# A planner's constants and priorities set anew, and one queue in it for all transfers

## The chip, the core and the metric

The kernel runs on one core of one Trainium2 chip. The core has five engines with an instruction list each, executed in order: TensorE (PE in the profile, with its weight loads shown apart as PEld), VectorE (DVE), ScalarE (ACT), GpSimd (POOL) and SyncE (SP). Here SP issues all plain transfers and POOL issues the transfers that add to their target. Engines wait for each other by semaphores. The metric is the device time of one execution in microseconds (us), the median of the runs shown; lower is better.

## What is computed

A graph network over 16 batches of 1024 nodes with 256 channels, in float32: three graph attention layers (4 heads, 1 head, 1 head) and one transformer layer with 8 heads of 32 channels. Every layer reads relu(layernorm(x)) and is added to x. One 1024 x 1024 adjacency matrix masks all of them. Cut to what matters:

```python
def gat(h, adj, W, a, H, alpha):           # layers 0, 1, 2
    q = (h @ W).reshape(B, N, H, D)
    e = (q @ a[:D])[:, :, None] + (q @ a[D:])[:, None, :]
    e = where(adj > 0, leaky_relu(e, alpha), -big)
    return act(softmax(e, axis=2) @ q)     # elu, relu, elu

def transformer(x):                        # layer 3
    q, k, v = split(x @ w_qkv)             # 8 heads of 32
    s = where(adj > 0, q @ k.T / sqrt(32), -1e9)
    x = layernorm(x + softmax(s) @ v) * ln1_g + ln1_b
    f = relu(x @ w1 + b1) @ w2 + b2
    return layernorm(x + f) * ln2_g + ln2_b

x = x + gat0(relu(ln(x))); x = x + gat1(relu(ln(x)))
x = x + gat2(relu(ln(x))); x = x + transformer(relu(ln(x)))
```

## The kernel before

A node set of 1024 is 8 tiles of 128 rows (NT), handled in two halves of 4 tiles (TH). The function `direct` does not write instructions in order. Its inner functions *record* pieces of work: `pe`, `act`, `dve`, `pool` and `dma` each append one `Work` with an engine, a duration in us, a function that emits the instructions, and the buffers that it writes and reads. A piece on PE is several matmuls, for instance eight of L840. From the buffers `Record.add` (L138) derives which work must precede which. A `Ring` of n buffers hands them out in turn; the four PSUM banks `bank` are `Shared`, handed out when the work is placed. The four banks `sc` are a ring.

`Record.schedule` (L170) is the planner. It keeps a clock for each engine, and repeatedly places the work that can start earliest; among several that are ready on an engine it takes the one with the lowest key. It adds the work's own duration, the price of a change of matmul form (`SWITCH`, with `turn` weighing it by `BIAS` in the choice), and the time that passes until others see the result (`PASS`). A transfer goes into the queue of the engine that issues it, `queue[e]`, which moves it in `moved` us and lets others see it `LANDING` later. The order in which work was placed is the order in which it is emitted, for each engine; the planner's times go nowhere else. So what a constant does to the kernel, it does through this order.

Keys come from `priority` (L117): each stream of work (a graph layer, the values, the attention steps, the feed-forward part) has a list of knots, `GATS`, `VALUES`, `STEPS`, `FEED`, in units of batches; the position in the stream is interpolated between them, and ACT's and DVE's work of a stream comes earlier by `LEAD`. Knots range over several units, so that the graph layers of a batch are placed beside the attention of batches before it.

The steps that the text comes back to, by lines of the kernel before:

- `gat`: transposes of the normalized half (L704, shown as L512), its copies (L710), projection (L716), exponentials of the scores (L727), score rows transposed (L782), copied (L788), stored to DRAM (`rd`, L789) and spread to all partitions (`row`, L797); masked weights `pt` on DVE (L813); products on PE, layer 0 in 32-column form (L927, L937), layers 1 and 2 in 128-column form (L840). A 32-column matmul uses a quarter of the array's columns, and four of them run side by side.
- `attention`: eight calls of `project` (L1070) a batch, in the order keys, queries, keys, queries, queries, keys, keys, queries. Each is a matmul pair (L1077) into a bank `sc`, a rounded copy `hi` on ACT (L1086), the rest `lo` on DVE (L1089), and 16 transfers of 64 KB (L1098) that stack them into `ks` or `qs`. `hi` and `lo` are rings of one buffer. `values` fills `sc` too (L1113).
- 32 attention steps a batch: scores into `sc` (L1295, four matmuls a step, in two pairs), exponentials (L1319), mask (L1328), products in 32-column form (L1161). The denominators come from `sums`: DVE adds two tiles (L1188), and POOL adds further ones by accumulating transfers of 512 KB (L1196).
- `feed`: transposes, two products (L1392), back, and the output.

Two lines of the planner that the change is about:

```python
                queue[e] = max(at + 0.2, queue[e]) + x.moved
                x.pass_on = queue[e] + LANDING - (at + us)
```

Of the kernel before, what the change touches and what calls it, by code (L numbers as in the profile page):

```python
# [16 lines left out]
AF = mybir.ActivationFunctionType  # L17
# [5 lines left out]
P = 128  # L23
# [75 lines left out]
PASS = {"pe": 0.22, "act": 0.18, "dve": 0.15, "pool": 0.13, "dma": 0.0}  # L99


class Work:


    def __init__(self, engine, us, emit, key, modes, moved):
        self.engine, self.us, self.emit, self.key, self.modes = engine, us, emit, key, modes
        self.pass_on = PASS[engine]
        self.moved = moved
        self.before = {}
        self.after = []  # L110
        self.shared = []
        self.opens = []
        self.ready = 0.0
        self.left = 0
# [10 lines left out]
class Record:  # L125
# [12 lines left out]
    def add(self, engine, us, emit, w=(), r=(), modes=("full", "full"), key=None, moved=0.0):  # L138
        stream = self.streams[-1]
        x = Work(engine, us, frozen(emit), key, modes, moved)  # L140
# [29 lines left out]
    def schedule(self):  # L170
# [8 lines left out]
        queue = dict.fromkeys(PASS, 0.0)  # L179
# [22 lines left out]
        def choose(e):  # L202
# [10 lines left out]
            if future[e] and (best is None or future[e][0][0] < best[0]):  # L213
                t, n, x = future[e][0]
                if opening(x) is not None:
                    t = max(t, at, opening(x))
                    best = min(best or (1e9,), (t, x.key + turn(x), n, x))
# [3 lines left out]
        while True:  # L221
# [18 lines left out]
            if x.moved:  # L240
                queue[e] = max(at + 0.2, queue[e]) + x.moved
                x.pass_on = queue[e] + LANDING - (at + us)
# [17 lines left out]
LANDING = 2.8  # L260
BIAS = 0.939
LEAD = {"act": 2.715, "dve": 0.501}

SWITCH = {
    ("full", "col4"): 0.095,
    ("full", "col2"): 0.095,
    ("qk", "full"): 0.104,
    ("qk", "col4"): 0.2,
    ("qk", "col2"): 0.2,
    ("col4", "full"): 0.135,  # L270
    ("col4", "qk"): 0.135,
    ("col4", "col2"): 0.135,
    ("col2", "full"): 0.1,
    ("col2", "qk"): 0.1,
# [3 lines left out]
def act_us(n, pointers=0):  # L278
    return (n / 1.2 + 65 + 93 * pointers) / 1000


def tt_us(n):
    return (n / 0.96 + 73) / 1000


def stt_us(n):
    return (n / 0.96 + 130) / 1000


def ts_us(n):  # L290
    return (n / 0.96 + 56) / 1000


def mm_us(n):
    return 2 * max(2 * n / 2.4 + 2.3, 109) / 1000
# [5 lines left out]
def direct(ctx, tc, flag, x, adj, gat_w, gat_a, w_qkv, ln1_g, ln1_b, ln2_g, ln2_b, w1, b1, w2, b2, out):  # L301
# [12 lines left out]
        (-3.456, -2.901, -1.928, -0.561, 0.293),  # L314
        (0.136, 0.471, 0.668, 0.738, 0.779),
        (0.851, 0.853, 0.845, 0.944, 1.195),
    )
    VALUES = (1.183, 1.195, 1.056, 1.638, 0.894)
    STEPS = (1.054, 1.508, 1.709, 1.977, 2.039)
    FEED = (2.172, 2.298, 2.316, 2.334, 2.401)  # L320
# [86 lines left out]
    def dve(us, emit, w, r):  # L407
        rec.add("dve", us, emit, w, r)
# [4 lines left out]
    def dma(moved, emit, w, r, key=None, us=0.44, engine="dma"):  # L413
        rec.add(engine, us, emit, w, r, key=key, moved=moved)

    def stats(src, src_ref, dst, dst_ref, whose="g"):
        st = r_st[whose].new()
        dve(0.342, lambda: nc.vector.bn_stats(st.t, src), [st], [src_ref])
        dve(0.11, lambda: nc.vector.bn_aggr(dst, st.t), [dst_ref], [st])
# [3 lines left out]
    def spread_of(srcs, src_refs, sums, squares, refs):  # L423

        act(0.19, lambda: nc.scalar.mul(sums, sums, -1.0 / C), refs, [])
        for k, (src, src_ref, ref) in enumerate(zip(srcs, src_refs, refs)):
            act(
                act_us(C, 1) + 60e-3,
# [51 lines left out]
    def normal(dst, dst_ref, src, src_ref, bias, scale, refs, func):  # L480
        act(
            act_us(C, 2),
# [5 lines left out]
    def watch(b_rec, view, k):  # L488
# [4 lines left out]
            0.3,  # L493
# [39 lines left out]
    def prepare(l):  # L533
# [5 lines left out]
            1.1,  # L539
# [7 lines left out]
            0.5,  # L547
            lambda: nc.sync.dma_start(
# [49 lines left out]
    def neighbours(it):  # L598
# [3 lines left out]
            1.9, lambda: nc.sync.dma_start(a_i, adj[it * P : (it + 1) * P, :]), [a32], []  # L602
# [39 lines left out]
    def setup():  # L642
# [3 lines left out]
        for it in range(NT):  # L646
# [5 lines left out]
            3.2,  # L652
            lambda: nc.sync.dma_start(wqkv_sb, w_qkv.rearrange("(t p) d -> p t d", p=P)),
# [12 lines left out]
        dma(5.0, load_feed, [b_feed], [], us=3.6)  # L666
# [4 lines left out]
    def gat(xt, b_mv, b_rstd, l):  # L671
# [8 lines left out]
        for hf in range(2):  # L680
# [30 lines left out]
            for k, it in enumerate(its):  # L711
                g = r_bank.new()

                def project():
# [11 lines left out]
                    0.184,  # L726
# [30 lines left out]
            if H == 1:  # L757
                act(
                    0.17,
# [5 lines left out]
                0.4,  # L765
# [10 lines left out]
        def turn_rows(hf):  # L776
# [11 lines left out]
            act(0.17, lambda: nc.scalar.copy(rt.t[:n, :], g.t[:n, :P]), [rt], [g])  # L788
            dma(0.15, lambda: nc.sync.dma_start(rd.t[:n, :], rt.t[:n, :]), [rd], [rt])  # L789
            return rd  # L790

        def spread(hf, h, rd):
# [3 lines left out]
                1.4,  # L796
# [31 lines left out]
        for hf in range(2):  # L828
            s = slice(hf * TH, (hf + 1) * TH)
            if H == 1:  # L830
                row = spread(hf, 0, rds[hf])
                pts = [weights(hf, 0, jt, row) for jt in range(NT)]
                for k in range(TH):
                    it = hf * TH + k
                    g = r_bank.new()
                    for j0 in range(0, NT, PART):
# [22 lines left out]
                        0.116,  # L859
# [12 lines left out]
                    if l != 1:  # L872
# [8 lines left out]
                            act_us(C),  # L881
# [10 lines left out]
                    else:  # L892
# [3 lines left out]
                        stt_us(C) + 60e-3,  # L896
# [15 lines left out]
            for h in range(0, H, 2):  # L912
                row = [spread(hf, h + u, rds[hf]) for u in range(2)]
                g, gd = r_bank.new(), r_bank.new()
                for jt in range(0, NT, 2):
# [7 lines left out]
                    def product():  # L923
# [23 lines left out]
                        3 * 0.855,  # L947
# [29 lines left out]
                def sums():  # L977
# [9 lines left out]
                dve(0.13, lambda: nc.vector.reciprocal(r, r), [ref], [])  # L987
# [11 lines left out]
                act(act_us(HALF), lambda: nc.scalar.activation(ex, o, AF.Exp), [b_ex], [b_o])  # L999
                act(  # L1000
                    act_us(HALF),
# [25 lines left out]
    def attention(b, xt, b_mv, b_rstd):  # L1027
# [42 lines left out]
        def project(g, hf, keys, stack, at):  # L1070
# [22 lines left out]
            for a in range(4):  # L1093
                part = ((hi, hi, lo, lo), (hi, lo, hi, lo))[keys][a]
                for r in range(HG):
                    dma(
                        0.33,
# [6 lines left out]
                        us=0.635,  # L1104
# [71 lines left out]
        for n in range(len(steps) + LAG):  # L1176
            m = n - LAG
            if m >= 0:
# [13 lines left out]
                elif jt % run:  # L1192
                    for ss, pt in zip(sums[g, hf], pas[m]):
                        dma(
                            3.0,
# [3 lines left out]
                            us=0.88,  # L1199
# [3 lines left out]
                    0.855,  # L1203
# [11 lines left out]
                if jt % run == run - 1:  # L1215
                    ss = pas[m] if run == 1 else sums[g, hf]
                    pe(
                        0.855,
# [11 lines left out]
            if m >= 0 and steps[m][2] == NT - 1:  # L1230
# [17 lines left out]
                def turned(u):  # L1248
# [5 lines left out]
                    0.17,  # L1254
# [26 lines left out]
            if n < len(steps):  # L1281
# [7 lines left out]
                for r0 in range(0, HG, GROUP):  # L1289
# [25 lines left out]
                    for r in range(r0, r0 + GROUP):  # L1315
                        pt, v, sc = pts[r // 2], r % 2, scs[r - r0]
                        act(
                            act_us(HALF),
# [22 lines left out]
    def feed(b, x3, hn):  # L1341
# [95 lines left out]
        def back(hf):  # L1437
            yT = yTs[hf]
            for it in (hf * TH, hf * TH + 2):
# [3 lines left out]
                    1.15,  # L1443
# [28 lines left out]
                for k in range(2):  # L1472
                    act(
                        act_us(C) + 60e-3,
# [15 lines left out]
                for k in range(2):  # L1490
# [23 lines left out]
                    0.65,  # L1514
                    lambda: nc.sync.dma_start(
# [13 lines left out]
    def batch(b):  # L1529
# [3 lines left out]
        for hf in range(2):  # L1533
            s = slice(hf * TH, (hf + 1) * TH)
            dma(
                2.0,
# [5 lines left out]
        for hf in range(2):  # L1542
            its = range(hf * TH, (hf + 1) * TH)
            for it in its:
                act(
                    act_us(C) + 60e-3,
# [17 lines left out]
        for hf in range(2):  # L1564
            s = slice(hf * TH, (hf + 1) * TH)
            dma(
                1.05,
# [623 lines left out]
```

## Time and profile before

| | |
|---|---|
| median of 3 runs | 4158.94 us (4154.15 to 4161.55) |
| span of the profiled execution, first to last instruction | 4150.3 us |
| PE busy | 4049.7 us, 98% |
| DVE busy | 3504.5 us, 84% |
| ACT busy | 2680.9 us, 65% |
| POOL busy | 558.7 us, 13% |
| mean granted clock of PE | 0.991 |

For the profiled execution the profile gives the span; no other time of that execution was kept. The median of the runs shown is 8.6 us above this span.

How to read it: busy time counts the instructions of an engine, without waits and without issuing transfers. PE's matmuls overlap and their ends are modelled, so the starts say more than the busy share. The views used are the page's first part, the waits (who waited for whom), the chain of work that ended last in order of time, and the timeline of one engine. Positions in an engine's list come from the two programs as they were built.

### The profile page before, as it was taken

The numbers are of one execution on the slowest core, as the hardware profiler recorded it, in microseconds if no ns is written. First come the engines' busy times: TensorE is split into PE (matmuls) and PEld (weight loads), VectorE is DVE, ScalarE is ACT, GpSimd is POOL, SyncE is SP. The second block draws the span as 40 slices with busy tenths as digits, with TensorE's granted clock in tenths as the row PEclk, the third lists the DMA queues.
The fourth block names the chain that finished last, engine by engine and source line by source line (L and its number), as shares of the span: only waits on it lengthen the run. The fifth ranks groups of instructions, "written<-read, shape, count | busy, mean of one in ns | idle before, by whom it ended". The sixth has DMA issues, their size and how long they took to land.

```text
span 4150.3 us, 68028 instructions
## 1 busy us (share of the span) xinstructions
PE 4049.7 (98%) x23874; PEld 2358.5 (57%) x23874; DVE 3504.5 (84%) x5994; ACT 2680.9 (65%) x6673; POOL 558.7 (13%) x631
## 2 busy tenths in 40 slices
PE   7899999999999999999999999999999999999998
PEld 3746556564665646556464665646556465564643
DVE  7498888988889898898988889888897988889866
ACT  4556667576766756667566665756667566575665
POOL 0001111111111101111111111111111111111110
PEclk9999999999999999999999999999999999999999
DMA  3124444344443424443254443434434244442441
GB/s 105 37 67 103 116 96 102 77 90 105 100 109 84 103 78 100 114 105 95 69 112 108 97 102 88 92 92 100 110 92 100 71 103 119 98 95 65 98 111 47
DMA packets 215246, 389.63 MB, mean 94 GB/s; under 512 B 45168, under 2 KB 80240, under 8 KB 214896
## 3 DMA queue, kind: packets, MB, share of 16 engines
q1 hardware_dynamic: 180336, 259.36, 22.3%
q0 software_dynamic: 34560, 125.84, 16.0%
q8 instruction: 190, 3.11, 0.3%
q14 instruction: 160, 1.31, 0.1%
HBM read 91.03 MB, written 33.95 MB: 30 GB/s over the span
## 4 chain that ended last, share of the span: by engine, by line
PE 79%; ACT 8%; DVE 6%; DMA 2%; SPq 2%; issue 2%; POOL 0%; DVEq 0%; ACTq 0%
PE bank L840 18%; PE bank L1161 12%; PE sc L1295 10%; PE bank L927 10%; PE bank L716 7%; PE bank L512 5%; PE bank L937 5%; PE bank L1392 5%; PE sc L1077 4%; ACT waste L429 2%; PE sc L1113 2%; SPq L1098 2%; DVE pa L1328 2%; ACT pa L1319 1%; DVE pt L813 1%
## 5 line engine op out<-in xcount | busy, mean ns | idle before, releaser
L1319 ACT ACTIVATE pa<-sc 128x512 f32<-128x512 f32 x2048 | 1108.1, 607 | 448.7 <-PE sc L1295 317.5
L1328 DVE TENSOR_TENSOR pa<-pa,mask 128x1024 f32<-128x1024 f32 x1024 | 1221.9, 1220 | 72.9 <-ACT pa L1319 68.6
L813 DVE SCALAR_TENSOR_TENSOR pt<-row,e,mask 128x512 f32<-128x512 f32 x1536 | 1068.1, 747 | 49.6 <-DMA row<-rd 35.8
L840 PE MATMUL bank<-qb,pt 128*128 128x257 f32 x4096 | 943.9, 383 | 1.4 <-DVE pt L813 1.0
L840 PEld LDWEIGHTS bank<-qb,pt 128*128 128x128 f32 x4096 | 780.5, 191 | 143.8 <-ACT pa L1319 11.7
L1295 PE MATMUL sc<-qs,ks 128*128 128x512 f32 x2048 | 702.8, 451 | 39.1 <-DVE lo L1089 35.7
L1295 PEld LDWEIGHTS sc<-qs,ks 128*128 128x128 f32 x2048 | 361.2, 190 | 288.1 <-issue 91.2
L1161 PE MATMUL bank<-pa,va 128*32 128x512 f32 x4096 | 514.7, 597 | 1.3 <-DVE pa L1328 1.0
L927 PE MATMUL bank<-pt,qb 128*32 128x512 f32 x4096 | 502.2, 596 | 4.3 <-DVE pt L813 3.4
L1188 DVE TENSOR_TENSOR sums<-pa,pa 128x1024 f32<-128x1024 f32 x360 | 435.6, 1221 | 30.3 <-PE bank L1161 25.3
L716 PE MATMUL bank<-w_aug,hT 128*128 128x259 f32 (+1 forms) x1536 | 391.2, 393 | 2.1 <-ACT hT L710 1.9
L1196 POOL DMA_DIRECT2D sums<-pa x240 | 210.5, 877 | 1059.4 <-DVE rec L860 239.0
L716 PEld LDWEIGHTS bank<-w_aug,hT 128*128 128x128 f32 x1536 | 283.9, 192 | 110.3 <-ACT pa L1319 12.6
L868 ACT ACTIVATE ex<-bank,rec 128x256 f32<-128x256 f32 x256 | 123.4, 482 | 303.3 <-DVE rec L860 302.6
L927 PEld LDWEIGHTS bank<-pt,qb 128*32 128x32 f32 x4096 | 122.3, 109 | 296.5 <-issue 224.0
L937 PE MATMUL bank<-pt,e 128*32 128x512 f32 x2048 | 278.6, 594 | 0.0
L1161 PEld LDWEIGHTS bank<-pa,va 128*32 128x32 f32 x4096 | 116.4, 109 | 256.7 <-issue 216.9
L1077 PE MATMUL sc<-hTa,wqkv_sb 128*128 128x512 f32 x512 | 244.5, 602 | 1.6 <-ACT pa L1319 0.8
L483 ACT ACTIVATE hn<-xt,mv,rstd 128x256 f32<-128x256 f32 x384 | 203.3, 597 | 51.6 <-DVE mv L456 30.0
L429 ACT ACTIVATE waste<-xt,mv 128x256 f32<-128x256 f32 x384 | 196.2, 511 | 7.0
L1161 PE MATMUL bank<-sums,ones 128*32 128x512 f32 x1440 | 193.5, 599 | 0.2 <-DMA sums<-pa 0.2
L1086 ACT CAST hi<-sc 128x512 fp32r<-128x512 f32 x128 | 74.5, 582 | 178.9 <-PE sc L1077 76.9
(119 smaller groups left out, 4305.9 us busy)
## 6 DMA issues: line engine op xcount, KB each, us to landing
sums<-pa POOLq DMA_DIRECT2D x240, 512.0 KB, 5.9
row<-rd SPq DMA_DIRECT2D x192, 256.0 KB
ks<-hi SPq DMA_DIRECT2D x512, 64.0 KB
ks<-lo SPq DMA_DIRECT2D x512, 64.0 KB
qs<-hi SPq DMA_DIRECT2D x512, 64.0 KB
qs<-lo SPq DMA_DIRECT2D x512, 64.0 KB
xt<-in_x_dram SPq DMA_DIRECT2D x32, 512.0 KB
x<-xt SPq DMA_DIRECT2D x32, 512.0 KB
```

Source lines behind the costliest of these rows:

```text
L429: lambda: nc.scalar.activation(waste.t, src, AF.Square, bias=sums[:, k : k + 1], accum_out=squares[:, k : k + 1]),
L716: nc.tensor.matmul(g.t[:, : C + 3 * H], hT.t[:, ct, k * P : (k + 1) * P], w_aug[l][:, ct, :], start=ct == 0, stop=ct == CT - 1,)
L813: lambda: nc.vector.scalar_tensor_tensor(pt.t, row.t, e3[:, 2, jt // TH, h, jt % TH : jt % TH + 1], mask[:, jt, hf * HALF : (hf + 1) * HAL ...
L840: nc.tensor.matmul(g.t[:, : D + 1], pts[jt].t[:, k * P : (k + 1) * P], qb[:, jt, 0, :], start=jt == 0, stop=jt == NT - 1,)
L927: nc.tensor.matmul(g.t[u * D + d : u * D + d + D3, :], qb[:, j, h + u, d : d + D3], pts[u][j - jt].t, start=j == 0, stop=j == NT - 1,)
L937: nc.tensor.matmul(gd.t[c : c + D3, :], one(jt + k, h + u).to_broadcast([P, D3]), pts[u][k].t, start=jt == 0, stop=jt == NT - 2,)
L1077: nc.tensor.matmul(sc.t, wqkv_sb[:, ct, c0 : c0 + P], hT.t[:, ct, hf * HALF : (hf + 1) * HALF], start=ct == 0, stop=ct == CT - 1,)
L1161: nc.tensor.matmul(ac.t[r * D3 : (r + 1) * D3, :], columns(r), of_head(r), start=first, stop=last,)
L1188: lambda: nc.vector.tensor_add(ss.t, p0.t, p1.t),
L1295: nc.tensor.matmul(scs[r - r0].t, ks.t[:, r, jt * P : (jt + 1) * P].bitcast(F32R), q.t[:, r, :].bitcast(F32R), start=True, stop=True,)
L1319: lambda: nc.scalar.activation(pt.t[:, v, :], sc.t, AF.Exp, scale=1.0 / math.sqrt(D3)),
L1328: lambda: nc.vector.tensor_mul(pt.t, pt.t, mask[:, jt : jt + 1, i0 : i0 + HALF].to_broadcast([P, 2, HALF]),),
```

## The change

Constants of the planner get other values: durations of ACT, DVE and POOL work, the prices of form changes, the times until others see a result, `BIAS`, `LEAD`, and all knots. `ts_us` halves its cost by element. ACT's cost gets a term for sources in SBUF. Each transfer gets its own time to land (`lands`), to which one `SLACK` is added, in place of the common `LANDING`. One queue holds the transfers of SP and of POOL; a transfer that is placed more than `AHEAD` before the queue's end keeps its engine for so much longer. And where the next work to become ready has no free bank, the planner looks further down the list for one that has. Which work is done, and the instructions of each piece, stay the same.

```diff
-PASS = {"pe": 0.22, "act": 0.18, "dve": 0.15, "pool": 0.13, "dma": 0.0}
+PASS = {"pe": 0.322, "act": 0.098, "dve": 0.189, "pool": 0.13, "dma": 0.0}
...
-        queue = dict.fromkeys(PASS, 0.0)
+        queue = 0.0
...
             if future[e] and (best is None or future[e][0][0] < best[0]):
-                t, n, x = future[e][0]
-                if opening(x) is not None:
-                    t = max(t, at, opening(x))
-                    best = min(best or (1e9,), (t, x.key + turn(x), n, x))
+                for t, n, x in sorted(future[e]):
+                    if opening(x) is not None:
+                        t = max(t, at, opening(x))
+                        best = min(best or (1e9,), (t, x.key + turn(x), n, x))
+                        break
...
             if x.moved:
-                queue[e] = max(at + 0.2, queue[e]) + x.moved
-                x.pass_on = queue[e] + LANDING - (at + us)
+                queue = max(at + (us if e == "pool" else 0.2), queue) + x.moved
+                us = max(us, queue - at - AHEAD)
+                x.pass_on = queue + x.lands + SLACK - (at + us)
...
-LANDING = 2.8
-BIAS = 0.939
-LEAD = {"act": 2.715, "dve": 0.501}
+AHEAD = 3.5
+SLACK = 0.492
+BIAS = 1.245
+LEAD = {"act": 5.831, "dve": -1.91}
 
 SWITCH = {
-    ("full", "col4"): 0.095,
-    ("full", "col2"): 0.095,
-    ("qk", "full"): 0.104,
-    ("qk", "col4"): 0.2,
-    ("qk", "col2"): 0.2,
-    ("col4", "full"): 0.135,
-    ("col4", "qk"): 0.135,
-    ("col4", "col2"): 0.135,
-    ("col2", "full"): 0.1,
-    ("col2", "qk"): 0.1,
+    ("full", "col4"): 0.137,
+    ("col4", "full"): 0.18,
+    ("qk", "col4"): 0.15,
+    ("col4", "qk"): 0.184,
+    ("qk", "full"): 0.016,
 }
 
-def act_us(n, pointers=0):
-    return (n / 1.2 + 65 + 93 * pointers) / 1000
+def act_us(n, pointers=0, sbuf=0):
+    return (n / 1.2 + 41 + 50 * sbuf + 101 * pointers) / 1000
...
 def ts_us(n):
-    return (n / 0.96 + 56) / 1000
+    return (n / 1.92 + 65) / 1000
...
     GATS = (
-        (-3.456, -2.901, -1.928, -0.561, 0.293),
-        (0.136, 0.471, 0.668, 0.738, 0.779),
-        (0.851, 0.853, 0.845, 0.944, 1.195),
+        (-3.83, -3.567, -2.52, -0.678, -1.262),
+        (0.004, 0.495, 0.516, 0.706, 0.869),
+        (0.85, 0.865, 0.865, 0.866, 1.578),
     )
-    VALUES = (1.183, 1.195, 1.056, 1.638, 0.894)
-    STEPS = (1.054, 1.508, 1.709, 1.977, 2.039)
-    FEED = (2.172, 2.298, 2.316, 2.334, 2.401)
+    VALUES = (1.414, -2.297, 0.107, 1.655, 0.953)
+    STEPS = (0.981, 1.432, 1.629, 2.113, 1.764)
+    FEED = (2.113, 2.25, 2.477, 2.246, 2.657)
...
-    def dma(moved, emit, w, r, key=None, us=0.44, engine="dma"):
-        rec.add(engine, us, emit, w, r, key=key, moved=moved)
+    def dma(moved, lands, emit, w, r, key=None, us=0.57, engine="dma"):
+        rec.add(engine, us, emit, w, r, key=key, moved=moved, lands=lands)
...
             pool(
-                0.4,
+                0.686,
...
                     dma(
-                        0.33,
+                        0.3,
+                        1.5,
                         lambda: nc.sync.dma_start(
                             stack.t[a * D3 : (a + 1) * D3, r, at : at + HALF],
...
-                        us=0.635,
+                        us=0.59,
...
                         dma(
-                            3.0,
+                            2.8,
+                            0.85,
                             lambda: nc.gpsimd.dma_start(ss.t, pt.t, accum_op=ALU.add),
...
-                            us=0.88,
+                            us=1.135,
```

## The prediction

> **What bounds the kernel now.** I read the page first: TensorE (PE) is busy for 98% of the span, and the chain that ended last is PE work for 79%.
>
> ```profile
> span 4150.3 us, 68028 instructions
> PE 4049.7 (98%) x23874; PEld 2358.5 (57%) x23874; DVE 3504.5 (84%) x5994; ACT 2680.9 (65%) x6673; POOL 558.7 (13%) x631
> ...
> PE 79%; ACT 8%; DVE 6%; DMA 2%; SPq 2%; issue 2%; POOL 0%; DVEq 0%; ACTq 0%
> ```
>
> No instruction is added or removed; each engine's list is put in another order. So I need what PE loses to order. Matmul ends are modelled, so I took starts. Back to back, matmuls start this far apart: L840 0.217 us, L1295 0.235, L1077 and L1392 0.429, transposes 0.109, four 32-column matmuls side by side 0.429. A visit to the 32-column form and back (another form before and after) costs 0.23 us over these spacings (median of 132 visits between 128-column work; the other kinds agree). I call the sum of spacings and visits in a list "PE work". From batch 2 to 13 the list repeats itself: one batch is 238.0 us of spacings and 26 visits, 244.0 us, and the first scores matmuls (L1295) of consecutive batches start 251.5 us apart (mean; 249.4 to 254.5). So 7.5 us of a batch are lost. Where? The waits of PE name one group:
>
> ```profile
> PE sc L1295 <- DVE lo L1089: 35.7, 14, 4.2
> PE bank L512 <- DVE pa L607: 15.3, 4, 12.7
> PE bank L512 <- ACT hn L483: 9.4, 12, 5.7
> ```
>
> The second and most of the third belong to the setup. The first comes once in a batch; in start times it is 14 gaps of 1.5 to 4.4 us over the 0.235, 40.6 us together. The chain of one of them, in order of time:
>
> ```profile
> 1828.73 0.59 SPq L1098
> 1829.32 0.04 issue
> 1829.36 3.56 DMA qs<-lo
> 1832.93 0.35 DVE xt L897 x2
> 1833.27 1.62 issue
> ...
> 1835.18 0.70 DVE lo L1089
> 1835.89 0.04 issue
> 1835.93 0.96 PE sc L1295 x3
> ```
>
> Each batch calls `project` eight times (numbers 0 to 7: keys, queries, keys, queries, queries, keys, keys, queries). Each fills one of four `sc` banks, which ACT (`hi`) and DVE (`lo`) read, and sends 16 transfers from `hi` and `lo`, which are single buffers. So `lo` of project 5 waits until the transfers of project 4 have landed; until it is written its bank is held, and PE stops at the fourth next user of a bank. The queue of SP is why they are late:
>
> ```profile
> 1833.05 4.10 SPq L1098 DMA_DIRECT2D ks<-hi  x4
> 1837.23 5.24 SPq L1098 DMA_DIRECT2D ks<-lo  x4
> 1842.52 2.49 SPq L1098 DMA_DIRECT2D ks<-hi  x4
> ```
>
> ```profile
> 1833.48 0.86 POOL L1196 DMA_DIRECT2D sums<-pa  x1 [2.68 <-DVE xt L897]
> 1836.74 0.86 POOL L1196 DMA_DIRECT2D sums<-pa  x1 [2.40 <-DVE lo L1089]
> ```
>
> Four transfers take SP 2.49 us, but 4.10 and 5.24 while POOL's accumulating ones are under way. The planner of before keeps a queue for each issuer and can't see this.
>
> **The change, part by part** (us, against the span).
>
> Durations. The new constants sit on the trace: between back-to-back starts L483 takes 0.492 (old 0.464, new 0.496), L727 0.126 (0.184, 0.126), L882 0.307 (0.278, 0.304), L897 0.343 (0.457, 0.342), L860 0.078 (0.116, 0.077). They cost nothing themselves; what they do is in the order.
>
> Visits. The new PE list has 409 visits to the 32-column form, the old 430: 21 x 0.23 = -4.8. Visits of L1295, whose form is as wide, cost -0.01 between 128-column work and are left out.
>
> Project 4 to 5. Measured from the start of project 4 (median of ten batches), its last transfer leaves SP at 16.5 and `lo` of project 5 is written at 22.0; the old list needs the bank at 15.1 + 4.1 = 19.2 of PE work. That is the gap: 2.8. The new list puts 19.5 us between the two and needs the bank at 23.6, and has one foreign transfer among those of project 4 instead of four. The room is 1.6 even at 22.0. All 40.6 go, and with them a follower that shows in the starts, 0.44 before the next scores x 14 = 6.2: -46.8. Bounds: 0, if the transfers slip by as much as project 5 does; -46.8.
>
> Project 6 to 7. This pair moves together, from 16.0 to 9.9; the bank is needed at 9.9 + 9.3 = 19.2 instead of 22.1. The old trace has `lo` of project 7 written at 19.3, and PE starts 0.15 after DVE where it waits for it (L1255 to L512): 0.25 x 14 = +4. Bounds: 0, if the transfers take 10.1 (16 x 0.63, as those of project 7) instead of the 14.0 measured; 22.0 as in the pair above, 2.95 x 14 = +41. I take 19.3, the same pair with POOL's transfers at nearly the same distance (first ones ready 5.5 before project 6, now 4.9).
>
> Project 5 to 6: needed at 23.1 (22.2 before); no gap before, none now.
>
> First scores of a batch. They move from 39.2 to 32.3 us of PE work after project 0. They need the 14th transfer of project 1, which now leaves SP at 35.2 to 35.8 and lands 2 to 3.6 later (3.56 in the chain above; 2.1 from project 6's last transfer to `lo` of project 7), 37.2 to 39.4. In the new list of SP 11 transfers fewer stand ahead of it (eight of project 2, two `row`, one `rd`), 11 x 0.63 = 6.9: 30.3 to 32.5. I take 0; bounds 0 and 0.2 x 15 = +3.
>
> Rows. The tightest way from the score transpose (L782) over `rd` and `row` to the first product goes from 13.0 to 10.5 us of PE work; in batch 0 the same way with less in between took 7.2 to the first `pt`. Hidden, 0.
>
> ACT and DVE lists. I summed the durations between each release by PE and the next use by PE along one or two engines. The old list has no place that is short; the new one has one a batch, 11 ACT instructions after a projection (L727 to L710), short by 0.35: x 14 = +5. Bounds 0, and +11, since the old list's tightest place (room 0.0) lost 0.42 in the trace.
>
> Setup, first and last batch. PE loses 60 us up to the first scores matmul (12.7 of it before the first matmul) and 21 in the last batch. The distances around layers 0 and 1 of the first batch are the old ones; the rest moves by some us both ways. 0, bounds -10 and +10, a sixth of the 60.
>
> Sum: -4.8 - 46.8 + 4 + 5 = -42.6, a span of 4107.7. The median of the three runs shown, 4158.9, is 8.6 above the profiled span; with that, 4116.
>
> A rule against it: a landing took 3.56 in the chain above. The Trainium skill, DMA: Bandwidth & Descriptors, section "Anatomy of one DMA — SWDGE (gpsimd) path", gives a transfer a fixed part of about 2.0 us that scales with nothing (it is a fit for transfers issued by GpSimd; these are SP's). By it `lo` of project 5 would be written at 16.5 + 2.0 + 0.7 = 19.2, when it is needed: the gap would not be the transfers' doing, the change would not remove it, and the sum would be +4, about 4163 (an estimate from that page). Here the measured landing decides.
>
> **The rivals.**
>
> A. The gap moves to project 7. For it: that pair was closed up by 6 us. Against: its transfers had 2.8 us of room before. At the bound of 22.0 the sum is -42.6 + 37 = -5.6: 4153.
>
> B. Slower: the first scores wait for their queries. If SP's 14th transfer of project 1 does not come forward (SP waits for `hi`, and `hi` for project 0's transfers, both ahead of it), it lands at 37.2 to 39.4 against 32.3: 4.9 to 7.1 x 15 = +74 to +107, so 4190 to 4223. It decides from 2.8 us a batch on (42.6 / 15), a landing at 35.1. Against: six of the eight `hi` transfers followed at 0.63 in the old trace, so SP and not `hi` set the pace.
>
> C. The order does nothing: the 7.5 us are matmul spacing that I priced too low, and come back anywhere. Then only the visits count: 4154. Against: 35.7 us are idle in the waits themselves.
>
> D. More is gained: DVE stands in line behind `lo` (18.3 us on `qs<-lo`, 14.9 on `ks<-hi` in its waits), and what it delays comes early too. The gap and its follower are 3.3 of the 7.5 lost in a batch; half of the other 4.2 x 14 = -29: 4087.
>
> **How the numbers follow.** Forecast 0.64, A 0.12, B 0.09, C 0.04, D 0.11. A change under 0.2% (8 us) can't be told from none: the three runs lie 0.18% apart. A's price slides from the forecast's 4116 to 4153, and only its upper half falls within 0.2%. Low end: D, 4087. High end: 4146, most of the way through A; B, C and the top of A, some 0.17, are left out. Faster holds the forecast, D and half of A, 0.81; same is C and the other half, 0.10; slower is B, 0.09.
>
> **What would show it.** Right: no PE wait for `lo` L1089 over a few us in sum; scores of consecutive batches some 248 us apart; 409 visits; SP's stretched transfers no fewer. Wrong: that wait stays (the slip of project 4), stands before another L1295 (A), a wait of L1295 for DMA `qs<-hi` or `qs<-lo` appears (B), or ACT's lists hold PE at L716 and L512 for over 1 us a batch. What would upset all of it is a wait in the repeated batch that no row of the old trace has, for it is paid 14 times.

## The result: no measurable change

The changed kernel takes 4160.15 us (median of 12 runs, 4154.52 to 4166.12), the kernel before 4158.91 (12 runs, 4152.69 to 4162.05): a ratio of 1.0003, 95% interval 0.9994 to 1.0011. The forecast was 4116, in a range of 4087 to 4146. The profiled span is 3.3 us longer. The page of the kernel after, its span, its engines, and the share of the engines in the chain that ended last:

```profile
span 4153.6 us, 68304 instructions
...
PE 4053.8 (98%) x23874; PEld 2365.0 (57%) x23874; DVE 3499.9 (84%) x5994; ACT 2682.1 (65%) x6673; POOL 550.6 (13%) x631
...
PE 52%; DVE 20%; ACT 9%; SPq 7%; DMA 6%; issue 5%; POOL 0%; DVEq 0%; ACTq 0%; POOLq 0%
```

The busy shares are as before, and so are the counts of each engine's instructions; the total differs (68028 before) in those that only wait or issue. The last line is not as before: TensorE was 79% of the chain and is 52%, and DVE has gone from 6% to 20%, SP's queue from 2% to 7%, DMA from 2% to 6%. So what set the end is now spread over transfers and what waits for them. The waits of TensorE (us in total, times, longest; L1300 is the old L1295, L930 the old L927, L1092 the old L1089, L511 the old L512):

```profile
PE bank L511 <- DVE pa L608: 14.1, 5, 10.9
PE sc L1300 <- DMA ks<-lo: 11.4, 9, 2.3
PE bank L930 <- DVE pt L816: 10.3, 24, 1.5
PE bank L718 <- ACT hT L712: 9.3, 19, 1.7
...
PE sc L1300 <- DVE lo L1092: 8.5, 12, 1.8
```

The wait for `lo` has come down from 35.7 to 8.5 us, and rows stand here that the old list did not have: scores that wait for a transfer into `ks`, products that wait for the weights `pt`. The third row is far too small. When a weight load waits, the matmuls behind it start late without an idle TensorE, and the load's own rows carry it. The waits of weight loads for `pt`, first before, then after:

```profile
PEld bank L927 <- DVE pt L813: 59.1, 102, 3.3
...
PEld bank L930 <- DVE pt L816: 144.8, 257, 2.0
```

Three of the ten between 2490 and 2504 us, in the timeline of weight loads:

```profile
2494.50 0.29 PEld L930 LDWEIGHTS bank<-pt,qb 128*32 128x32 f32 x8 [0.56 <-DVE pt L816]
...
2499.12 0.16 PEld L930 LDWEIGHTS bank<-pt,qb 128*32 128x32 f32 x8 [0.76 <-DVE pt L816]
...
2502.89 0.16 PEld L930 LDWEIGHTS bank<-pt,qb 128*32 128x32 f32 x8 [1.06 <-DVE pt L816]
```

From start to start (over the spacing that the quickest fifth of the same work keeps in both traces) the products of layer 0, L930 and L940, lose 51.8 us; before, 13.7. That is +38, nearly all that the forecast had gained. It is paid in every batch: first scores of consecutive batches, 1 to 13, are 252.0 us apart (249.3 to 254.4), and were 251.5.

**Where it comes from.** I followed one batch backwards, first scores at 2487.5. DVE's timeline, the instructions that waited:

```profile
2485.32 0.17 DVE L440 TENSOR_SCALAR rstd<-mv 128x4 f32<-128x4 f32 x1 [2.12 <-ACT waste L428]
2486.62 0.17 DVE L455 TENSOR_TENSOR mv<-mv,rstd 128x4 f32<-128x4 f32 x1 [1.13 <-POOL rstd L448]
2489.12 0.69 DVE L1092 TENSOR_TENSOR lo<-sc,hi 128x512 f32<-128x512 f32 x1 [2.34 <-DMA ks<-hi]
```

DVE stands still for 2.12 us on ACT and for 2.34 on a transfer, just before the products need `pt`. ACT's timeline says what ACT waited for:

```profile
2478.01 0.42 ACT L1555 ACTIVATE waste<-xt 128x256 f32<-128x256 f32 x1 [2.12 <-DMA xt<-in_x_dram]
...
2482.30 0.59 ACT L1089 CAST hi<-sc 128x512 fp32r<-128x512 f32 x1 [1.93 <-DMA qs<-lo]
```

Transfers again: the load of the next nodes, and the halves (the 64 KB transfers of L1102) of project 1, which must leave `hi` before project 2 may write it. Behind this cast stand the squares (L428, for a variance of the layer norm) that DVE waited for. SP issued these in one close line (two `row`, halves of project 0, the 512 KB load, halves of project 1):

```profile
2467.59 1.03 SPq L800 DMA_DIRECT2D row<-rd  x2
2468.66 1.15 SPq L1102 DMA_DIRECT2D ks<-hi  x2
...
2473.01 0.43 SPq L1545 DMA_DIRECT2D xt<-in_x_dram  x1
2474.35 6.12 SPq L1102 DMA_DIRECT2D qs<-hi  x8
```

Two things are late here against the planner. Issues are slow: the eight `qs` halves of the last line shown took 6.12 us, where the planner reckons 0.59 for one and 4.7 for eight (this is the slowest of ten batches, which take 4.94 to 6.12, in the mean 5.3). And data land late: the moment at which a transfer's semaphore completes, against the planner's own time for it (mean of ten batches, both counted from the batch's first scores), is 0.87 us late for the second `row`, 1.56 for the `ks` halves behind it, 2.07 for the `qs` halves behind the load, 3.2 for the `ks` halves after those. No accumulating transfer moves there. In a second place, 120 to 140 us after the first scores, accumulates do move, and the issues themselves are slow:

```profile
2610.12 4.68 SPq L1102 DMA_DIRECT2D ks<-hi  x4
2614.89 1.55 SPq L1102 DMA_DIRECT2D ks<-lo  x1
```

```profile
2608.25 0.86 POOL L1201 DMA_DIRECT2D sums<-pa  x1 [1.65 <-DVE sums L1192]
2611.98 0.86 POOL L1201 DMA_DIRECT2D sums<-pa  x1 [2.87 <-DVE pt L816]
2615.79 0.86 POOL L1201 DMA_DIRECT2D sums<-pa  x1 [2.95 <-DVE rec L863]
```

Here the scores wait for the last halves of project 5 (the row `ks<-lo`, 11.4 us), and later for `lo` of project 7.

### The profile page after: what moved, and what is told of

It reads as the page before. It is cut to its first block, busy times and chain, and to the rows that moved or that the text cites. A ratio compares the mean times of both kernels' runs of the same rounds, so it can differ in the third digit from the quotient of the medians.

```text
span 4153.6 us, 68304 instructions
## 1 busy us (share of the span) xinstructions
PE 4053.8 (98%) x23874; PEld 2365.0 (57%) x23874; DVE 3499.9 (84%) x5994; ACT 2682.1 (65%) x6673; POOL 550.6 (13%) x631
## 4 chain that ended last, share of the span: by engine, by line
PE 52%; DVE 20%; ACT 9%; SPq 7%; DMA 6%; issue 5%; POOL 0%; DVEq 0%; ACTq 0%; POOLq 0%
PE bank L1165 9%; PE bank L843 9%; DVE pt L816 7%; PE bank L930 7%; DVE pa L1333 7%; PE sc L1300 6%; SPq L1102 6%; PE bank L718 5%; PE bank L511 4%; PE bank L1397 4%; PE bank L940 3%; ACT pa L1324 2%; PE sc L1117 2%; DMA sums<-pa 2%; DMA ks<-lo 2%
## 5 line engine op out<-in xcount | busy, mean ns | idle before, releaser
L843 PEld LDWEIGHTS bank<-qb,pt 128*128 128x128 f32 x4096 | 768.6, 189 | 202.6 <-issue 49.4
L1300 PE MATMUL sc<-qs,ks 128*128 128x512 f32 x2048 | 701.9, 450 | 20.8 <-DMA ks<-lo 11.4
L930 PE MATMUL bank<-pt,qb 128*32 128x512 f32 x4096 | 550.7, 596 | 13.7 <-DVE pt L816 10.3
L1300 PEld LDWEIGHTS sc<-qs,ks 128*128 128x128 f32 x2048 | 362.5, 188 | 209.8 <-ACT pa L1324 63.2
L718 PE MATMUL bank<-w_aug,hT 128*128 128x259 f32 (+1 forms) x1536 | 381.5, 392 | 9.3 <-ACT hT L712 9.3
L718 PEld LDWEIGHTS bank<-w_aug,hT 128*128 128x128 f32 x1536 | 286.3, 191 | 115.8 <-ACT hT L712 19.0
L930 PEld LDWEIGHTS bank<-pt,qb 128*32 128x32 f32 x4096 | 135.2, 109 | 335.2 <-issue 167.6
L940 PE MATMUL bank<-pt,e 128*32 128x512 f32 x2048 | 322.2, 592 | 0.0
L463 POOL TENSOR_TENSOR rstd<-rstd,neg_half 128x4 f32<-128x4 f32 x64 | 102.1, 1596 | 829.5 <-DVE rstd L460 829.5
L428 ACT ACTIVATE waste<-xt,mv 128x256 f32<-128x256 f32 x384 | 195.3, 509 | 9.0
```

What stands on the lines that cost most here:

```text
L718: nc.tensor.matmul(g.t[:, : C + 3 * H], hT.t[:, ct, k * P : (k + 1) * P], w_aug[l][:, ct, :], start=ct == 0, stop=ct == CT - 1,)
L843: nc.tensor.matmul(g.t[:, : D + 1], pts[jt].t[:, k * P : (k + 1) * P], qb[:, jt, 0, :], start=jt == 0, stop=jt == NT - 1,)
L930: nc.tensor.matmul(g.t[u * D + d : u * D + d + D3, :], qb[:, j, h + u, d : d + D3], pts[u][j - jt].t, start=j == 0, stop=j == NT - 1,)
L940: nc.tensor.matmul(gd.t[c : c + D3, :], one(jt + k, h + u).to_broadcast([P, D3]), pts[u][k].t, start=jt == 0, stop=jt == NT - 2,)
L1300: nc.tensor.matmul(scs[r - r0].t, ks.t[:, r, jt * P : (jt + 1) * P].bitcast(F32R), q.t[:, r, :].bitcast(F32R), start=True, stop=True,)
```

## Experiments

Theory T: the new list is as short as forecast where transfers land when its planner thinks; on the chip they are later in two places of each batch (by 0.87 to 3.2 us in the first), and the waits reach TensorE. Rivals: S, the loss is in spacings of TensorE that were priced too low; V, DVE simply has too much work there. Times are medians of two to eight runs; the kernel before ran beside each group (4154.65 to 4161.94 us).

### Smaller transfers, same order

The planner's durations are left alone, so every engine executes the very list of the changed kernel; only bytes are cut.

```diff
-                    row.t,
-                    rd.t[h * TH : (h + 1) * TH, :]
+                    row.t[:, :P],
+                    rd.t[h * TH : h * TH + 1, :]
```

> The changed kernel with the same order of instructions on every engine; each transfer of a row of attention terms moves only a quarter (128 of 512 columns, 64 KB for 256 KB), the rest of the row tiles holds ones, so the output is not the reference's. Theory T (the order's transfers land later than the planner reckons, the vector engine has no spare time at the start of a batch, so its weights pt come late and TensorE's products wait): rows land about 1 us earlier and the key and query transfers behind them 1.5 to 2 us earlier, the waits of L930 for pt shrink from 1.9 + 0.75 us a batch to under 1, time 4120 to 4137 (25 to 40 off 4160). Rival S (the loss is in spacings of TensorE that the sum priced too low, and transfers are covered): 4155 to 4165.

```diff
-   stack.t[a * D3 : (a + 1) * D3, r, at : at + HALF],
-   part.t[r * D3 : (r + 1) * D3, :],
+   stack.t[a * D3 : (a + 1) * D3, r, at : at + P],
+   part.t[r * D3 : (r + 1) * D3, :P],
```

> The changed kernel with the same order; each of the 2048 transfers of halves to qs and ks moves a quarter (16 KB for 64 KB), the rest of the tiles holds zeros, so the output is not the reference's. Theory T: the stretched issues on SP's queue (1.2 to 1.7 us instead of 0.59) become rarer, the waits of the casts and of lo for the earlier transfers fall, TensorE's waits of L1300 for ks and lo (1.4 of the drift of 4.6 us a batch) go, and part of those for pt: 4115 to 4140. Rival S: 4155 to 4165. Rival V (the vector engine alone is overloaded at the start of a batch, whatever the transfers do): the waits for pt stay, only those of L1300 go: 4138 to 4148.

```diff
-   nc.gpsimd.dma_start(ss.t, pt.t, accum_op=ALU.add)
+   nc.gpsimd.dma_start(ss.t[:, 0, :256], pt.t[:, 0, :256], accum_op=ALU.add)
```

> The changed kernel with the same order; each of GpSimd's 240 accumulating transfers adds a quarter (128 KB for 512 KB), so the output is not the reference's. Theory T: the stretched issues of the keys 120 to 135 us after a batch's first scores go, and with them 1.8 us a batch: 4130 to 4140; the waits for pt at the batch's start, where no accumulate moves, stay at 2.3 us a batch. Rival S: 4155 to 4165.

All three edits in one kernel:

> The three cuts together, same order; output not the reference's. Theory T: the batches come down from 251.8 to 247.2 to 248.5 us, 3.3 to 4.6 us in 13 batches, time 4095 to 4118. Rival S: over 4150. Rival V: 4125 to 4140, with L930's waits for pt unchanged.

| | us | ratio to before (95%) | period of a batch | slow issues |
|---|---|---|---|---|
| changed kernel | 4160.2 | 1.0003 (0.9994 to 1.0011) | 252.0 | 189 |
| x1_rows | 4143.0 | 0.9959 (0.9937 to 0.9982) | 250.8 | 194 |
| x2_stack | 4120.2 | 0.9897 (0.9855 to 0.9940) | 249.5 | 171 |
| x3_acc | 4126.2 | 0.9916 (0.9888 to 0.9945) | 249.8 | 62 |
| x4_all | 4099.9 | 0.9848 (0.9806 to 0.9891) | 248.3 | 64 |

(Slow issues: of SP's 2048 issues of halves, those over 0.85 us; the median of all is 0.59, the mean of the slow ones 1.36.)

S falls: 60 us go without one matmul changed. x4_all lies in T's range, x2_stack too; rows gave less than expected (17 us for 25 to 40), accumulates more (34 for 20 to 30). x3_acc shows that the accumulates make most of SP's slow issues: 189 fall to 62. The wait of weight loads for `pt`, 144.8 us in the changed kernel, is 116.8 in x1_rows, 111.4 in x2_stack, 154.9 in x3_acc and 98.5 in x4_all. So it depends on the plain transfers, which rival V had excluded, and not on the accumulates. x4_all's period of 248.3 is about the 248 that the prediction expected of the new list. What is left of the waits there (L934 and L1304 are L930 and L1300):

```profile
PE bank L934 <- DVE pt L820: 6.7, 11, 1.5
...
PE sc L1304 <- DVE lo L1096: 3.3, 3, 1.5
```

The scores' wait for `ks<-lo` is gone. But of the 2.6 us that the products of layer 0 lose in a batch, 1.4 stay.

### Is it DVE's load?

```diff
-   nc.vector.tensor_add(ss.t, p0.t, p1.t)
+   nc.vector.tensor_add(ss.t[:, :, :P], p0.t[:, :, :P], p1.t[:, :, :P])
```

> The changed kernel, its own order, with the vector engine's 360 adds L1192 cut to a quarter of their columns, which takes about 0.8 us off each, 290 us in all (the sums' other columns hold ones; output not the reference's). Rival V (the vector engine has too much work around the batch's start): the waits of L930 for pt go, 4125 to 4140. Theory T (it stands still for late transfers there, 22 to 24 of 100 us, and is full only 17 to 110 us after the first scores, where TensorE does not wait): the waits stay, 4145 to 4162.

4161.1 us, ratio 1.0011 (0.9999 to 1.0023): nothing gained, and the wait for `pt` stands as it was (L932 is L930):

```profile
PE sc L1302 <- DMA ks<-lo: 13.9, 10, 2.0
...
PE bank L932 <- DVE pt L818: 10.4, 23, 1.5
```

V falls. The busy time in stretches of the changed kernel's batch (us of the stretch, then PE, PEld, DVE, ACT, POOL busy, clock, DMA share, GB/s) agrees:

```profile
2440.00:2461.00 21.00, 20.36 (x108) 11.46 (x100) 13.00 (x32) 17.77 (x55) 6.81 (x8) 1.00 0.73 163
2461.00:2500.00 39.00, 38.60 (x254) 19.30 (x256) 28.87 (x59) 23.71 (x57) 3.79 (x6) 1.00 0.47 123
2500.00:2550.00 50.00, 49.85 (x376) 21.93 (x370) 48.84 (x85) 24.09 (x56) 3.03 (x4) 1.00 0.16 44
```

Around the first scores at 2487.5 DVE works 28.87 of 39 us; it is full after 2500, where TensorE loses nothing to it.

### Bytes, or the pace of SP?

I first took the load of 512 KB, still whole in x4_all, for the cause of what is left.

```diff
-   lambda: nc.sync.dma_start(xt.half(hf), x_b[:, s, :]),
+   lambda: nc.sync.dma_start(xt.half(hf)[:, : TH if b < 2 else 1, :], x_b[:, s, :][:, : TH if b < 2 else 1, :]),
```

> The changed kernel with the same order; from batch 2 on each load of the next nodes brings a quarter (128 KB for 512 KB), the rest of the tile keeps older nodes, so the output is not the reference's. The products of layer 0 (L930, L940) lose 2.6 us a batch to late pt in the changed kernel and 1.4 in x4_all. Theory T (the load delays the moments that wait for it and the halves of project 1 issued behind it): the loss falls to 0.8 to 1.8 us a batch, time 4135 to 4150. Rival W (what is left in x4_all is the order of ACT and DVE, not the load): the loss stays over 2.2, time 4153 to 4165.

> x4_all with the load cut as well; output not the reference's. Theory T: the loss of the products of layer 0 falls from 1.4 to under 0.5 us a batch, the batches to 246.8 to 247.6 us, time 4078 to 4092. Rival W: the loss stays over 1.0, time 4094 to 4102 as x4_all.

4161.8 us (1.0010, 0.9995 to 1.0026) and 4099.5 (0.9857, 0.9826 to 0.9889): nothing is gained, and the loss at the products stays at 1.4 us a batch. T missed in both, and W's ranges held. In x6_load_all the load lands 2.2 us ahead of the planner's time, and yet the last `qs` half that `hi` waits for is 0.84 late, the last of all 1.9: the delay grows from issue to issue. From start to start, halves that follow each other leave SP 0.633 us apart in the median; in the mean 0.651 there and 0.707 in the changed kernel. So the issues themselves were cut:

```diff
-   lambda: nc.sync.dma_start(
+   lambda: r % 2 == 0 and nc.sync.dma_start(
```

> x4_all with every second of the 2048 issues of halves left out, so that SP is never behind (output not the reference's). Theory P (SP's pace: 0.633 to 0.65 us an issue for the planner's 0.59, over 27 issues in a row 1.2 to 1.6 us late): the products of layer 0 lose under 0.5 us a batch instead of 1.4, batches 246.5 to 247.6 us apart, time 4076 to 4092. Rival W (the order of DVE and ACT): they lose over 1.0, time 4094 to 4102.

> The changed kernel with every second issue of the halves left out, the rest whole (output not the reference's). It halves their bytes and their issues, where x2_stack (4120) quartered the bytes and kept the issues. Theory P: the issues count, so it is faster than x2_stack, 4085 to 4112. Rival W: bytes alone count, 4115 to 4140.

x7_all_issues: 4076.1 us, 0.9795 (0.9766 to 0.9823), batches 247.0 us apart. x8_issues: 4084.3, 0.9815 (0.9786 to 0.9843), 247.6. The loss at the products of layer 0 falls to 0.2 us a batch in both. x8_issues moves more bytes than x2_stack (half for a quarter) and is 36 us faster. So bytes alone do not explain it, and rival W falls: the order of DVE and ACT is the same in x7_all_issues. What counts is how many issues stand in SP's line. How the 76 us of x8_issues divide between fewer issues and fewer bytes was not measured, nor was an issue's time on SP told apart from what its transfer costs those in flight beside it. The wait of weight loads for `pt` in x8_issues is below that of before (L932 is L930):

```profile
PEld bank L932 <- DVE pt L818: 51.7, 84, 2.0
```

The chain's share by engine in x7_all_issues, whose span of 4073.3 is the planner's own 4075:

```profile
PE 93%; ACT 3%; DVE 3%; DMA 1%; issue 0%; POOL 0%; SPq 0%; DVEq 0%; ACTq 0%
```

### What was the old wait?

The same cuts in the kernel before, its own order.

> The kernel before, its own order, with the same three cuts as x4_all (rows, halves and accumulates move a quarter of their bytes; output not the reference's). The wait for lo that the prediction removed is a chain of 16 issues of 0.59 us and a landing, which loses little by smaller transfers. Theory T: most of that wait stays, 4125 to 4145, so the new order is 25 to 45 us the better one where transfers land in time. Rival S: the new order is worth nothing of its own, 4092 to 4108 as x4_all's 4100.

> The kernel before, its own order, with GpSimd's 240 accumulates alone cut to a quarter of their bytes (output not the reference's). Theory T2 (the accumulates in flight stretch SP's issues from 0.59 to about 1.36 us, project 4's sixteen issues so take 13.9 us instead of 9.4 to 10, and that, not the order, was the wait for lo that the prediction removed): stretched issues fall from 226 to about 60, PE's waits for lo from 35.7 to under 8 us, time 4112 to 4128. Rival (the bytes of the halves and rows themselves make the chain that long): the waits for lo stay over 25 us, 4140 to 4155.

b4_all: 4094.0 us, ratio 0.9840 (0.9821 to 0.9860). b3_acc: 4099.0, 0.9859 (0.9839 to 0.9878). T missed on b4_all, and rival S held: with transfers out of the way the old order is as short as the new one (4094.0 against 4099.9), so under these cuts the new order has no worth of its own (x7_all_issues, without SP's pace, is another 18 us below b4_all; its twin in the old order was not run). And the accumulates alone were the old wait: without three quarters of their bytes 56 us are gone, and the wait of 35.7 us for `lo` with them (T2 had its cause right and its gain too small, 4112 to 4128). With the same cut the new order takes 4126.2 (x3_acc): its own loss, at a batch's start, is not the accumulates' doing. TensorE's waits in b3_acc, its lines those of before:

```profile
PE bank L512 <- DVE pa L607: 15.3, 4, 12.8
PE bank L512 <- ACT hn L483: 9.6, 13, 5.7
...
PE sc L1295 <- ACT pa L1319: 3.5, 7, 0.9
...
PE sc L1295 <- DVE lo L1089: 0.7, 2, 0.4
```

The transfers of project 5 in the timeline of SP's queue, which took 4.10 and 5.24 us for four before (2.49 is the quick rate):

```profile
1812.73 2.41 SPq L1098 DMA_DIRECT2D ks<-hi  x4
1815.23 2.44 SPq L1098 DMA_DIRECT2D ks<-lo  x4
1817.72 3.59 SPq L1098 DMA_DIRECT2D ks<-hi  x4
1821.35 2.49 SPq L1098 DMA_DIRECT2D ks<-lo  x4
```

My figure for the chain was off, though. Project 4's last issue ends 15.5 us after its start, and 16.5 before, a gain of 1.0, not the 4 that I expected; `lo` of project 5 is written at 19.0 instead of 22.0, so the other 2.0 us came off the landing.

### One part of the change alone

The new durations, mode costs and queue, with `BIAS`, `LEAD` and all knots of before:

> One part of the change alone: new durations, mode costs and the one queue, with the priorities and lead times of the kernel before. By its own durations this planner's list ends at 4283 us (the changed kernel's at 4075). Theory T (the list's end by those durations plus what transfers add): 4285 to 4340. Rival P (the durations are the gain, the new priorities lose it): under 4140.

4397.1 us (one run), 57 over the top of T's range. Rival P falls all the same: the old priorities under the new durations and queue are 237 us slower than the kernel before.

### A list that keeps its length

If what a list loses is what its transfers come late, the planner should be told longer plain transfers, and the priorities be chosen for lists that still hold when transfers in flight share the engines. I fitted such sharing to the landings in the traces of before and after (estimates of that fit, which no run measures by itself: while they overlap, a row weighs 2.9 times a half and an accumulate 5.2 times; an issue of SP takes 1.08 us while an accumulate moves), replayed candidate lists with it, and kept the shortest. The edit, with n3_plan's values:

```diff
-AHEAD = 3.5
-SLACK = 0.492
+AHEAD = 1.334
+SLACK = 0.744
...
-                1.2,
+                1.227,
...
-                        0.3,
+                        0.54,
...
-                            2.8,
+                            2.687,
...
-                    1.0,
+                    1.676,
```

(a row, a half, an accumulate, and a load of the second norm, whose store goes from 0.65 to 1.089), with other knots, `BIAS` and `LEAD`. An accumulate is a little shorter in all four (2.652 to 2.79), and in n1_plan a half is too (0.18 for 0.3).

> The changed kernel with the planner told longer transfers (rows 1.361 for 1.2 us, loads and stores of the second norm 1.85 times as long, an issue that waits for the queue from 2.1 us of backlog) and priorities chosen for an order that keeps its length when transfers share the engines; by the planner's own durations the list ends at 4095, 20 later than the changed kernel's. Theory T: what a list loses on the chip is what its transfers come late, so this one loses little: 4095 to 4135. Rival: any list chosen on a planner's arithmetic loses it again on the chip: 4145 to 4170.

> As n1_plan, from another start of the choice of priorities (rows 1.284 us, halves 0.533, list's end by the planner 4096). Theory T: 4095 to 4140. Rival: 4145 to 4170.

> As n2_plan, the choice of priorities carried further (rows 1.227 us, halves 0.54, loads and stores of the second norm 1.676 times, backlog from 1.334 us; the planner's own end 4090). Theory T: 4088 to 4115; not over n2's 4100 by more than 15. Rival (n2 was a lucky draw among lists): 4120 to 4160.

> As n3_plan from another branch of the choice; the planner's own end 4089.5. Theory T: 4088 to 4115. Rival (n2 was a lucky draw): 4120 to 4160.

| | list's end by its own planner | span on the chip | difference | median us, ratio to before (95%) |
|---|---|---|---|---|
| kernel before | 4099.9 | 4150.3 | +50.4 | 4158.91 |
| changed kernel | 4075.1 | 4153.6 | +78.5 | 4160.2, 1.0003 |
| z2_oldprio | 4283.0 | 4395.3 | +112.3 | 4397.1 (one run) |
| n1_plan | 4095.2 | 4125.0 | +29.8 | 4127.5, 0.9919 (0.9902 to 0.9935) |
| n2_plan | 4095.7 | 4096.8 | +1.1 | 4099.7, 0.9852 (0.9836 to 0.9869) |
| n3_plan | 4090.2 | 4092.1 | +1.9 | 4092.9, 0.9844 (0.9828 to 0.9861) |
| n4_plan | 4089.5 | 4078.4 | -11.1 | 4080.5, 0.9817 (0.9800 to 0.9833) |

The four last are faster than both kernels, n4_plan by 1.8%, with all bytes moved. Its plan is 14 us longer than the changed kernel's and its span 75 us shorter. n4_plan is 8 us below its range, the others lie in theirs. How far one list does better than another was not foreseen: n1_plan looked as good as n2_plan. No run tells the longer times and the new priorities apart; n1_plan, whose halves are the short ones, gained least. The page of n4_plan, and its chain's share:

```profile
span 4078.4 us, 68086 instructions
...
PE 4008.3 (98%) x23874; PEld 2349.8 (58%) x23874; DVE 3498.5 (86%) x5994; ACT 2684.9 (66%) x6673; POOL 580.8 (14%) x631
...
PE 88%; ACT 4%; DVE 3%; DMA 2%; SPq 2%; issue 1%; POOL 0%; DVEq 0%; ACTq 0%
```

TensorE is 88% of the chain, more than before the change, and its own waits for `lo` and `pt` are small (that for `hT` stays, 8.9 for 9.3):

```profile
PE bank L511 <- DVE pa L608: 11.0, 1, 11.0
PE bank L718 <- ACT hT L712: 8.9, 18, 1.6
...
PE bank L930 <- DVE pt L816: 6.7, 6, 2.4
...
PE sc L1300 <- DVE lo L1092: 2.1, 2, 1.9
```

n4_plan has as many slow issues as the kernel before (223 for 226), and the same pace of SP as the changed kernel (0.633 median, 0.711 mean). It does not move its transfers faster; it does not need them so soon. Its batches are 246.9 us apart (246.7 to 248.0).

## Why the prediction was wrong, point by point

| step | forecast | measured |
|---|---|---|
| Visits | -4.8 | 430 and 409 in the lists executed; no run prices them alone |
| Project 4 to 5 | -46.8 | the wait is gone: a late `lo` of project 5 costs 0.85 us, once, in the last batch |
| Project 6 to 7 | +4 | 4.7 us idle (8 waits in batches 1 to 14) |
| First scores of a batch | 0 | no wait for their queries |
| ACT lists, L727 to L710 | +5 | L718 waits 9.3 for `hT`, 1.9 before: +7.4 |
| Rows, first products | 0 | +38 in starts of L930 and L940, setup included |
| Project 5 to 6 | 0 | `lo` in time, but scores wait 11.4 us for project 5's halves |
| Setup, last batch | 0 | first scores 1.2 us later, and 1.5 us more from the last batch's first scores to the end |

- *What bounds the kernel* was read rightly, its cause only in part. SP's queue beside the accumulates was named, and b3_acc shows that they make the whole wait. I then treated the lateness as a property of one pair of `project` calls that more distance cures. In these traces any transfer comes late that stands behind or beside many others, and the new list brought others close together.
- *The step that failed* is the rows' "Hidden, 0", for the products that need `pt`: they lost 38 us. I compared distances in TensorE's work with the time that the same way took in the old trace. That time is no constant: it depends on how many issues stand in SP's line at that place. The new list puts two rows, two rounds of halves and a load into one line of some 27 issues, with one short stop (0.9 us in the batch shown, until `hi` of project 1 is written). At 0.633 to 0.71 us each for the planner's 0.59, its end is 1 to 3 us late by this estimate, and the halves behind it landed 3.2 us late. With half of the issues left out (x8_issues, which halves the bytes of the halves too) the loss at these products falls from 2.6 to 0.2 us a batch; with the rows' own bytes cut (x1_rows) most of the wait for `pt` stays, 116.8 of 144.8 us. I had used 0.63 for the first scores, and did not ask the same of the rows and of `hi`.
- *The ACT and DVE lists* were summed by durations, between a release by TensorE and its next use. Releases by transfers were left out of that sum, and it is these that hold up `hi`, `lo` and the means and variances of the norm, in engines that execute in order, before `pt` is due.
- *Rivals.* The time fell just above C (4154) and the top of A (4153), by neither: the gap did not move to project 7 (A, at +37), spacing was not at fault (C). B did not come. Of its signs, SP's slow issues were forecast no fewer and fell from 226 to 189. The last sentence of "What would show it" named what happened, a wait in the repeated batch that no row of the old trace has, but gave it no price and, outside B, no chance.
- *The page's rule of a fixed part of about 2.0 us* (the Trainium skill, DMA: Bandwidth & Descriptors, "Anatomy of one DMA — SWDGE (gpsimd) path") is a fit for transfers that GpSimd issues; the middle of the landings of SP's halves, counted from the start of the issue, agrees with it: 1.99 to 2.47 us by kind of half in the trace before. The gap that it would have denied was real, and went with the accumulates' bytes (in b3_acc `lo` of project 5 is written at 19.0, beside the 19.2 of the rule). What decides here is the tail, one landing in twenty over 3.4 to 5.6 us by kind, and the pace ahead of it.
- The terms in the table add up to more than the 3.3 us by which the span grew: some 9 us were gained in other places, which I did not trace one by one.

## What to carry to other kernels

A list scheduled by a planner is worth what is left of it when its transfers come late: compare the list's own end with the chip's (here +78 us for the shorter list, -11 for the longer), and look first at the share of the critical engine in the chain that ended last. When work is moved, count the issues that stand in line ahead of each transfer at their measured pace, ask what it will now fly beside, and follow a late landing through the in-order engines to the next user, not only to its own. Cutting a transfer's bytes, or leaving out issues, with the order kept is a cheap test of which of the two costs.

## What the runs showed of the hardware

- SP's pace is a resource: 64 KB halves in a line leave it 0.633 us apart in the median, 0.707 in the mean of the changed kernel. Half as many issues (with half of the bytes) took the changed kernel from 4160 to 4084 us, a quarter of the bytes with all issues to 4120.
- An accumulating transfer of 512 KB in flight slows the issue of plain ones: of SP's 2048 issues of 64 KB, 189 (changed kernel) and 226 (before) took over 0.85 us for a median of 0.59; with accumulates of 128 KB, 62 and 60. With rows or halves cut instead, still 194 and 171. Of the halves that the kernel before issued while an accumulate was in flight 184 of 422 were slow, of the others 42 of 1626.
- A landing takes longer in a close line of transfers. In the changed kernel a row of 256 KB landed in 3.1 us alone, in 3.2 with another row 1.3 us behind it, and two rows in a line of halves 0.6 us apart, halves ahead of them and behind, in 4.2 and 5.0. With rows of 64 KB (x1_rows) it was 3.1 and 3.2 at that same place. The Trainium skill, DMA: Bandwidth & Descriptors, section "Queues, rings and completion order", says that a DMA engine works off one queue's ring in order and takes turns between queues by packets. No run here separates what stands ahead of a row from what follows it, so these landings neither confirm nor deny that.
- A late operand of a weight load hardly shows in TensorE's own idle time: 10.3 us for L930 in the waits of PE, 144.8 in those of its weight loads (59.1 before), and 38 more lost in starts by L930 and L940 together.
